# Two transformer layers on one core: the same instructions, put in order by the scheduler with its timeline simulation

## The chip, the core and the metric

The kernel runs on one core of a Trainium2 chip. The metric is the device time of one execution in microseconds (us), taken outside the profiler; less is better. A core has five engines that matter here: PE (matrix products; PEld is its loading of weights, which overlaps the products), DVE (vector work), ACT (activations and copies), POOL (general vector work) and SP, which here only issues DMAs. Each engine works through its own list of instructions strictly in order; an instruction that needs another engine's result waits for a semaphore, and everything behind it on its engine waits too.

## The reference

The input x holds 4 sequences (b) of 256 tokens with 256 features, in float32. Two layers follow, each an attention block and a feed-forward block with a residual:

```
x = x + attention0(layernorm(x))   # 16 query heads, 8 key/value heads of 128, RMS norm and rotary
                                   # embedding of q and k, causal with a window of 128
x = x + ffn0(layernorm(x))         # (silu(x Wg) * x Wu), the two largest of every four kept, then W_down; 1024 wide
x = x + attention1(layernorm(x))   # 16 heads of 128, causal
x = x + ffn1(layernorm(x))         # fwht(silu(x W1^T) * x W3^T) W2^T; fwht is a Walsh-Hadamard transform over 1024
```

All matrix products are in float32.

## The kernel before

The kernel is written in a framework of tiles: the program names buffers and emits instructions in the order in which its Python code runs; the framework finds out which instruction needs which, gives buffers of a pool out in turn, adds the waits, and **a scheduler orders the instructions of each engine** from an estimate of how long each takes. So the order on an engine is not the order of the code. Two things bind it besides the data: a buffer can only be written again when its readers are done, and `tc.issue_after(instruction)` keeps the instructions of a block behind one that the code names. Tiles carry the number of their buffer (sc_5554), which is the same in both programs. 

**Attention, both layers.** The work is cut into 16 units: in layer 0 unit n is sequence b = n // 4 and head group g = n % 4 (four query heads, two key/value heads); in layer 1 it is group n // 4 and sequence n % 4. `pipelined` (line 300 on) emits the stages of different units side by side: in layer 0 the seven stages project, rotate, turn, score, split, join, attend run 0, 0, 1, 2, 3, 4, 4 steps behind; in layer 1 project, score, attend run 0, 1, 2 behind. Each unit has two halves (kk), and each half goes through one chain:

- `sc`, the scores of two heads, on PE (L213, L214): a 128x128 and a 128x256 product for each head
- `p` and its row maxima `mx`, mask added, on DVE (L216); `nb`, the negative maxima scaled, on DVE (L221, L223)
- the exponential in place on ACT, four instructions (L226); `rs`, one over the row sums, on DVE (L231)
- four scalings of `p` by `rs` on POOL (L234), then `pl` on POOL (L240): the float32 words taken apart into planes of 16 bits, 128x1536
- `plT`, the planes transposed by a DMA that SP issues (L249); `pT`, the halves put together again on ACT and DVE (L260)
- `av` (line 268 and 271 in layer 1, 394 and 398 in layer 0) on PE; `zT`, its copy, on ACT (L731, L402)
- `po` on PE (L280 in layer 1, as `po1`; L292 in layer 0) and `x += po` on DVE (L286, L297)

In layer 0 the queries and keys come from `pj` on PE (L446); DVE multiplies by the rotary tables (`qs`, `qc`, L451) and adds (L469); ACT squares (L456), DVE sums (`ss`, L470); POOL makes `r`, the factor of the norm, with a power (L483 to L489), and scales k (`qc`, L492); PE turns k (`tr_k`, L518). The queries go to the scores turned by PE (`tr_q`, copied by DVE at L508) or, for later units, by DMA (`qpl` L240, `qplT` L480, put together by DVE into `qT` at L512). The layer norms are `bn_stats`, `bn_aggr` on DVE (L151, L152), a power on POOL (L157), `xn` on DVE (L171), and `tr_n` on PE (L182) or planes and a DMA transpose.

In layer 1 q, k and v come from `seven_products`: products of sums of 128-wide blocks, seven where plain blocks need eight. Each product (`qk_x`, `qk_y`, `qk_z`, L783; `v_x`, L789) is copied by ACT or summed by DVE (L654, L660, L663) before the same bank takes the next one.

**Feed-forward, both layers.** ffn0 makes gate and up (`pgu`, L550), keeps two of four on DVE (L569 to L583) and multiplies by W_down (`po_f`, L595). ffn1 makes both factors in the seven products (`gu_x`, `gu_y`, `gu_z`, L858), SiLU on ACT (L873), the product `h1` on DVE (L874), `po_f` (L595), then `x += po_f` (L604) and the output DMA.

The late part of layer 1's attention matters for the change. The output projections of units 9, 10, 11 and 13 (`po1` of the tiles 5577, 5588, 5650 and 5661) are not emitted at their turn but in the `attend` of units 14 and 15, behind the last projection:

```
        zTs, kept = {}, {14: (9, 10), 15: (11, 13)}

        def attend(n, held):
            ps, v = held
            for m in kept.get(n, ()):
                out(m, True)(zTs)
...
                    with tc.issue_after(last_of[1].ins):
                        project_out1(st([P, NT, D], "po1"), done[n], gw[g][2], b)
```

So PE has products at hand that need nothing more, which the scheduler may put where it likes behind the last projection. Unit 15's scores are sc_5524 and sc_5529 (p_5519) and sc_5549 and sc_5554 (p_5544); its two `av` are av1_5676 and av1_5685.

The change touches one line of `kernel`, where the framework's context is opened.

## Time and profile before

| | before |
|---|---|
| device time, 3 runs | 738.79, 738.90, 739.01 us; median 738.9 |
| span of the profiled execution, first to last instruction | 737.2 us |
| what lies around the span (median less span) | 1.7 us |
| granted PE clock, mean | 1.000 |
| PE, PEld busy | 725.0, 594.6 us |
| DVE, ACT, POOL busy | 469.2, 406.9, 345.0 us |

The profiled execution has no device time of its own beside its span; the runs' median less the span, 1.7 us, is taken as what lies around it. A PE that is busy is not a PE without loss: its matmuls are pipelined and a record's duration overlaps the next one, so the prediction goes by the distance from one start to the next. Two records stand in the trace for each float32 product, one for each transpose.

The stages of the kernel by time, from the trace: layer 0's attention to about 260 us, its feed-forward to about 360, layer 1's attention to about 655, its feed-forward to the end.

### The profile page before, as it was taken

Reading aid. Unit: us, or ns where it says so; the run is one execution under the profiler, and the core shown is the slowest. Engines: PE = TensorE matmul, PEld = TensorE weight load, DVE = VectorE, ACT = ScalarE, POOL = GpSimd, SP = SyncE. Lnnn points to the kernel's source line nnn. Section 1 sums busy time; section 2 is a strip of 40 time slices with the busy share of each in tenths; the row PEclk is TensorE's granted clock in tenths of the full one; section 3 lists DMA queues with packets and bytes.
Section 4 is the critical chain, followed back from the end, with each engine's and each line's share of the span. In section 5 each row is a group of like instructions: output and inputs, shape, how many; then the busy total and the mean of one; then the engine's idle time right before and its main releaser. Section 6 shows DMA issues by size and latency. Waiting matters only on the chain.

```text
span 737.2 us, 11593 instructions
## 1 busy us (share of the span) xinstructions
PE 725.0 (98%) x3912; PEld 594.6 (81%) x3912; DVE 469.2 (64%) x1402; ACT 406.9 (55%) x983; POOL 345.0 (47%) x489
## 2 busy tenths in 40 slices
PE   9999999999999999999999999999999999999998
PEld 5556576666666778888898999999998999899997
DVE  6999878888887537987655644464442655464443
ACT  2487887667767952222355555555556576434332
POOL 1588878897799631011116433343336575520000
PEclk9999999999999999999999999999999999999999
DMA  8732344425445545001324532342232223401100
GB/s 327 293 64 51 57 93 81 92 52 93 90 79 96 77 114 180 16 14 26 119 72 77 127 55 44 70 129 46 44 72 44 44 44 44 88 15 22 23 14 30
DMA packets 138348, 57.51 MB, mean 78 GB/s; under 512 B 131504, under 2 KB 133680, under 8 KB 137520
## 3 DMA queue, kind: packets, MB, share of 16 engines
q1 hardware_dynamic: 138288, 56.77, 33.9%
q8 instruction: 31, 0.51, 0.3%
q14 instruction: 29, 0.24, 0.1%
HBM read 22.94 MB, written 1.05 MB: 33 GB/s over the span
## 4 chain that ended last, share of the span: by engine, by line
PE 75%; DVE 9%; POOL 7%; issue 4%; ACT 3%; DMA 2%; SPq 0%; POOLq 0%; DVEq 0%; ACTq 0%
PE pj L446 10%; PE pgu L550 7%; PE po L292 7%; PE po_f L595 7%; PE qk_x L783 5%; PE po L280 5%; PE sc L214 5%; PE gu_x L858 4%; PE av L394 3%; PE qk_y L783 3%; PE v_x L789 3%; PE sc L213 3%; PE av L268 2%; POOL p L234 2%; PE gu_y L858 2%
## 5 line engine op out<-in xcount | busy, mean ns | idle before, releaser
L234 POOL TENSOR_SCALAR p<-p,rs 128x128 f32<-128x128 f32 (+1 forms) x256 | 115.4, 470 | 153.2 <-DVE rs L231 147.9
L240 POOL TENSOR_SCALAR pl<-p 128x1536 uint16<-128x1536 uint16 x64 | 94.3, 1474 | 4.8 <-POOL p L234 0.5
L260 ACT COPY pT<-plT 128x1536 uint16<-128x1536 uint16 (+1 forms) x60 | 86.2, 1494 | 11.5 <-DMA plT<-pl 11.5
L216 DVE CUSTOM_DVE_ANT_0 p<-sc,cst 128x128 f32<-128x128 f32 (+1 forms) x256 | 79.7, 351 | 10.5 <-PE sc L214 8.1
L226 ACT ACTIVATE p<-p,nb,r 128x128 f32<-128x128 f32 (+1 forms) x128 | 68.2, 535 | 20.2 <-DVE nb L223 20.2
L446 PE MATMUL pj<-wq,xnT 128*128 128x512 f32 x128 | 61.1, 595 | 1.1 <-DVE qT L508 1.1
L446 PE MATMUL pj<-wkv,xnT 128*128 128x512 f32 x128 | 60.1, 592 | 0.0
L226 ACT ACTIVATE p<-p,nb 128x128 f32<-128x128 f32 (+1 forms) x128 | 56.3, 447 | 4.0 <-DVE nb L221 4.0
L292 PE MATMUL po<-wo,zT 128*128 128x256 f32 x256 | 57.9, 379 | 0.0
L280 PE MATMUL po<-w_o,zT 128*128 128x256 f32 x256 | 57.6, 379 | 0.0
L456 ACT ACTIVATE sq<-pj 128x512 f32<-128x512 f32 (+1 forms) x64 | 30.9, 489 | 42.7 <-DVE qc L451 42.4
L292 PEld LDWEIGHTS po<-wo,zT 128*128 128x128 f32 x256 | 48.3, 190 | 7.0 <-ACT kT L519 0.6
L280 PEld LDWEIGHTS po<-w_o,zT 128*128 128x128 f32 x256 | 47.7, 190 | 6.0
L156 POOL TENSOR_SCALAR ve<-mv 128x2 f32<-128x2 f32 (+1 forms) x17 | 4.3, 253 | 97.5 <-DVE mv L152 97.0
L446 PEld LDWEIGHTS pj<-wkv,xnT 128*128 128x128 f32 x128 | 24.3, 190 | 30.2 <-issue 28.0
L451 DVE TENSOR_TENSOR qs<-pj,sin_s 128x512 f32<-128x512 f32 (+1 forms) x64 | 35.3, 551 | 13.5 <-PE pj L446 12.9
L446 PEld LDWEIGHTS pj<-wq,xnT 128*128 128x128 f32 x128 | 23.5, 190 | 24.2 <-issue 19.9
L666 ACT COPY qk<-qk_x 128x512 f32<-128x512 f32 x16 | 9.4, 587 | 58.1 <-PE qk_x L783 58.1
L268 PE MATMUL av<-pT,v 128*128 128x256 f32 x128 | 38.4, 382 | 1.2 <-DVE nb L221 1.1
L214 PE MATMUL sc<-kT,qT 128*128 128x256 f32 x128 | 38.3, 381 | 0.0
L214 PE MATMUL sc<-qk 128*128 128x256 f32 x128 | 38.2, 380 | 0.0
L240 POOL TENSOR_SCALAR qpl<-qc 128x1024 uint16<-128x1024 uint16 x20 | 28.8, 1453 | 18.9 <-PE av L398 8.2
(151 smaller groups left out, 1748.8 us busy)
## 6 DMA issues: line engine op xcount, KB each, us to landing
w<-in_w_dram SPq DMA_DIRECT2D x3, 1024.0 KB, 4.7
wq<-in_wq_dram SPq DMA_DIRECT2D x4, 512.0 KB, 7.6
wkv<-in_wkv_dram SPq DMA_DIRECT2D x4, 512.0 KB, 8.4
wo<-in_wo_dram SPq DMA_DIRECT2D x4, 512.0 KB, 10.2
w_qk<-in_w_q_dram SPq DMA_DIRECT2D x4, 512.0 KB, 5.2
w_qk<-in_w_k_dram SPq DMA_DIRECT2D x4, 512.0 KB, 6.1
w_v<-in_w_v_dram SPq DMA_DIRECT2D x4, 512.0 KB, 7.3
w_o<-in_w_o_dram SPq DMA_DIRECT2D x4, 512.0 KB, 6.0
```

What stands on the lines that cost most here:

```text
L214: nc.tensor.matmul(sc[:, P : 3 * P], lhsT=q[:, P:T], rhs=k, start=True, stop=True)
L216: last_of["mx"] = nc.vector.tensor_tensor_reduce(out=p[:, j, cols], in0=sc[:, cols], in1=mask[:, cols], scale=1.0, scalar=-3.0e38, op0=ALU ...
L226: last_of["exp"] = nc.scalar.activation(p[:, j, cols], p[:, j, cols], AF.Exp, bias=nb[:, j, i : i + 1], scale=SCALE1 if rq is None else rq ...
L234: nc.gpsimd.tensor_scalar(p[:, j, cols], p[:, j, cols], rs[:, j, i : i + 1], 1.0, ALU.mult, ALU.mult)
L240: last_of["planes"] = nc.gpsimd.tensor_scalar(o, i, 1.0, 1.0, ALU.mult, ALU.mult)
L260: copy(words.rearrange("p (n w) -> p w n", w=2), halves[:, :, js].rearrange("p w j n -> p w (j n)"),)
L268: nc.tensor.matmul(av, lhsT=v0, rhs=pT[:, 0:T], start=True, stop=False, skip_group_check=True)
L280: nc.tensor.matmul(po[:, t, :], lhsT=zT[:, j, t * P : (t + 1) * P], rhs=w[:, j, :], start=(t == j == 0), stop=(j == 3), skip_group_check=True,
L292: nc.tensor.matmul(po, lhsT=zTs[hd // 4][:, hd % 4, t * P : (t + 1) * P], rhs=w[:, hd, :], start=(hd == 0), stop=(hd == n - 1),)
L446: last_of[0] = nc.tensor.matmul(pj, lhsT=xnT[:, c, t * P : (t + 1) * P], rhs=w[:, g, c, :], start=(c == 0), stop=(c == NC - 1),)
L550: nc.tensor.matmul(o[:, j, :], lhsT=w[:, c, f0 + j, :], rhs=xnT[:, c, :], start=(c == 0), stop=(c == NC - 1),)
L783: last_of[1] = nc.tensor.matmul(o[:, j, :], lhsT=wqk[i - 1][:, j // 2, j % 2, :], rhs=x[i - 1], start=(first and j == 0), stop=True, skip_ ...
```

## The change

The scheduler is told to order the instructions with its own timeline simulation instead of its default estimate of durations.

```diff
-    with tile.TileContext(nc) as tc:
+    with tile.TileContext(nc, schedule_with_timeline_sim=True) as tc:
         two_layers(tc, *args)
```

The compiled programs hold the same instructions with the same buffers: 2026 on PE, 1402 on DVE, 727 on ACT, 492 on POOL, 136 on SP. Their order differs on every engine, and with it the waits: side by side, the two lists of PE differ in 1481 lines, those of DVE in 2253, of ACT in 1128, of POOL in 477 and of SP in 41. The blocks under `issue_after` stay behind the instructions that they name.

## The prediction

> **What bounds the kernel now.** I read the page's head first, then PE alone: the change moves instructions and removes none, so it can only add or remove time in which PE stands still.
>
> ```profile
> span 737.2 us, 11593 instructions
> ...
> PE 725.0 (98%) x3912; PEld 594.6 (81%) x3912; DVE 469.2 (64%) x1402; ACT 406.9 (55%) x983; POOL 345.0 (47%) x489
> ...
> PE 75%; DVE 9%; POOL 7%; issue 4%; ACT 3%; DMA 2%; SPq 0%; POOLq 0%; DVEq 0%; ACTq 0%
> ```
>
> PE is busy for 98%. Since a matmul's record overlaps the next, I count PE's need by starts, in the timeline of PE:
>
> ```profile
> 628.48 0.38 PE L213 MATMUL sc<-qk 128*128 128x128 f32 x2
> 628.70 0.60 PE L214 MATMUL sc<-qk 128*128 128x256 f32 x2
> 629.13 6.64 PE L280 MATMUL po<-w_o,zT 128*128 128x256 f32 x30
> ...
> 646.22 0.38 PE L271 MATMUL av<-pT,v 128*128 128x128 f32 x2
> 646.73 0.70 PE L268 MATMUL av<-pT,v 128*128 128x256 f32 x2
> ```
>
> Two records 128 wide take 0.22 us to the next start, two 256 wide 0.43; 646.22 to 646.73 is 0.51, a stall of 0.29. Over the trace the medians of one record are 0.112 (128), 0.216 (256) and 0.430 us (512 wide), and 1888 x 0.112 + 1695 x 0.216 + 328 x 0.430 = 718.6 us. The first matmul starts at 1.2, the last ends at 734.2. So 18.5 of 737.2 us are not PE's own work; gaps over 0.12 us number 20 and sum to 11.3. **About 10 us is all that any order could win.** Who ends the waits:
>
> ```profile
> PE av L394 <- DVE mx L216: 2.1, 3, 0.8
> PE tr_k L518 <- POOL qc L492: 2.0, 2, 1.6
> PE idle L140 <- DVE zeroes L137: 1.2, 1, 1.2
> PE pj L446 <- DVE qT L508: 1.1, 2, 0.9
> PE av L268 <- DVE nb L221: 1.1, 1, 1.1
> PE qk_x L783 <- DVE qk L663: 0.4, 1, 0.4
> ```
>
> (us in total, times, longest.) By place: 1.76 at 20.5 us; 1.4 at 37-49; 1.0 at 71; 0.4 at 82-84; 1.2 at 147-150; 2.3 at 217-254, the end of layer 0's attention; 1.8 at 363-396, the start of layer 1's; 0.3 at 646.
>
> [...]
>
> **The change, part by part.** I set PE's instructions one behind the other at these step times, without gaps, in each program's compiled order, and call the position T. Its end, 718.7, is the same in both. A stall appears where the chain behind a PE result needs longer than the PE work that stands before its user (its cover). For DVE, ACT and POOL, too, one instruction costs its distance to the next start where the trace has them back to back: L216 0.20 (128 wide) and 0.34 (256), L451 0.60 (512) and 0.33 (256), L469 0.87, L512 0.75, L226 0.38 and 0.49, the four of L234 1.6, L240 1.45. Between such places nothing is lost: in most of layer 0 the cover from pj to tr_k to sc to av grows by some us, ffn0 keeps its order, and in the middle units of layer 1 pT comes about 0.1 us late at worst, where before's own order gives 0.1 to 0.3 late by the same count without a gap in its trace. These, and PE's moved projections in ffn0, I take at nothing, covered by PE's 40.00 of each 40 us; if that cover is too thin, see the rivals. SP's queue I take at nothing too: its transposes keep their order behind the planes.
>
> 1. Start (T 0-60). One pj block (1.7 us) now stands between tr_q and tr_k, against the gap of 1.76. But bn_stats and bn_aggr of x4 to x7 (4 x 0.34 + 4 x 0.08 = 1.7 us) stand earlier on DVE, and DVE is the tight one there:
>
> ```profile
> 20.00:60.00 40.00, 37.29 (x155) 22.81 (x155) 38.75 (x108) 25.75 (x73) 27.99 (x38) 1.00 0.46 149
> ```
>
> (PE 37.29, then PEld, DVE 38.75 of 40 us.) DVE's worst lag behind PE grows from 5.4 to 6.4 us. Bounds -1.8 and +1.5; taken **+0.5**, nearest to DVE's lag.
>
> 2. 147-150. POOL has r and qc ahead of the scalings of p, and xn 4 us more: **-1.2** (bounds -1.2, 0).
>
> 3. The next batch's first score (sc_1645, T 155.3). It waits for qT_1564, two copies on DVE. Before, they stood right behind the row maxima. Now DVE has ahead of them the rotation of unit 10 and x2 += po_1585, and that po is the block that ends on PE at T 155.3. So after it: 0.1, the addition 0.42, the first copy 0.75: 156.6, +1.3. The other way round, DVE's sum from the last maximum at T 149.9 (2 x 0.87, 3.7 for eight L451, 0.2, then 0.42 and 0.75) gives 156.7. Taken **+1.4** (bounds +1.0, +2.3).
>
> 4. End of layer 0's attention. From the last score to its av 12.1 us of cover stand where 17.3 stood; the chain would end about 1.1 late, while the four gaps of 2.3 lose their cause, their pT copies being ahead. **-1.2** (bounds -2.3, +1.1).
>
> 5. Start of layer 1's attention. The pT copies get 2 to 4.5 us of cover: -1.8; three new tight places (0.1, 0.3, 0.1): **-1.3** (bounds -1.8, +1.0).
>
> 6. **End of layer 1's attention**, the term that decides. Positions T:
>
> ```
>                               before           after
> sc_5529 ends                  613.5            620.4
> sc_5554 (last score) ends     614.8            624.8
> po1_5650, last 7 products     within 623.9-627.4   621.1-624.1
> av1_5676 starts               630.9            630.9
> av1_5685 starts               632.2            632.2
> ```
>
> The free projections, which before stood between the last scores and their av, now stand ahead of the last scores. Cover from the last score to av1_5685 falls from 17.4 to 7.4 us. What the chain needs is shown by before's chain of waits (start, us):
>
> ```profile
> 636.63 1.47 POOL pl L240
> 638.11 1.61 POOL p L234 x4
> ...
> 641.88 3.72 DMA plT<-pl
> 645.60 0.02 issue
> 645.62 1.06 ACT pT L260
> 646.68 0.04 issue
> 646.73 0.70 PE av L268 x2
> ```
>
> Maxima 0.7, nb 0.15, four exponentials 1.85, rs 0.2, scalings 1.6, planes 1.5, transpose 3.7, copy 1.1: 10.8 from score to av, 3.4 more than the cover. The queues make it a little worse: on DVE rs_5523 stands behind x6 and x7 += po1_5650, which ends at T 624.1. So rs 624.9-625.1, scalings to 626.7, planes 628.2, transpose 631.9, copy 633.0: av1_5676 is 2.1 late. The second half: POOL free at 628.2, scalings 629.8, planes 631.3, transpose 635.0, copy 636.1: av1_5685 3.9 late in all. Behind the waiting av stand two projections, then ffn1; none can pass. Less the 0.3 that goes at 646: **+3.5** (bounds +2.0, +5.0).
>
> 7. Tail (T 708-713). Blocks of po_f that separated the last products are moved ahead. gu_x_6190's last product must wait for L663's reading of its bank (0.1 + 0.69 + issue, about 0.9), and po_f_6216 for h1_6182, whose copy 0.59, SiLU 1.06, the L663 ahead and product 1.23 end at T 713.0 against 711.8. Together **+1.2** (bounds 0, +1.5); before shows no gap here.
>
> Sum: 0.5 - 1.2 + 1.4 - 1.2 - 1.3 + 3.5 + 1.2 = +2.9. Span 737.2 + 2.9 = 740.1; with the 1.7 between span and median, **741.8 us**.
>
> [...]
>
> **Rivals.**
> A, faster: the order mends the queues of DVE and POOL. Every gap but the first start is ended by DVE, POOL or a pT copy; if all 10 us go and terms 3, 6 and 7 cost their 6.4, the time is 738.9 - 10 + 6.4 = 735.3. For it: terms 2, 4, 5 are seen to lose their cause. Against: at 37-84 (2.8 us) DVE is full, and more DVE work stands early there. It decides once over 7.9 us of the gaps go (6.4 plus the 1.5 of 0.2%).
> B, nothing that a measurement can tell (0.2%, 1.5 us): PE has 718.6 of work in any order, terms 1 to 5 give -1.8, and 6 and 7 give 3 instead of 4.7: 737.2 - 1.8 + 3 + 1.7 = 740.1. For it: PE's 98%. Against: term 6's chain has 3.4 us more than its cover without any queue.
> C, slower still: the order leaves nothing spare. In layer 1's dozen middle units the margin is about -0.1 us; if each half unit is 0.1 to 0.3 late, 24 x 0.2 = 5 us come on top: 746.6. For it: po moved ahead of where it covered; against: PE 40.00 of 40 there before, at like margins.
>
> **How the numbers follow.** Forecast with its own range (740.4 to 744.5) 0.42; C (to 749) 0.18; B 0.20; A (to 735) 0.20. The range takes the cases to 736.0, where half of A is left out, and to 749. Chances: faster by over 0.2% 0.20, within 0.2% 0.20, slower 0.60.
>
> **What would show it.** Right: a PE wait of 1.5 to 4 us at the last two av of L268 with plT and pT on the chain before it; a wait of about 1.4 at sc <- DVE qT L512; none left at tr_k, av L394 at 147-254 or at 363-396. Wrong: PE without a gap at the end of layer 1's attention (then POOL or the transpose took less than before's rows), or many small gaps at L268 between 400 and 600 us (C).

## The result, and the profile after

| | before | after |
|---|---|---|
| device time, median of 4 runs on the same chip | 738.95 us (738.79 to 739.58) | 762.42 us (760.17 to 764.21) |
| ratio, with its 95% interval | | 1.0316 [1.0291, 1.0341] |
| span of the profiled execution | 737.2 us | 758.9 us (its own device time 760.65) |
| granted PE clock, mean | 1.000 | 0.993 |

The change costs 23.5 us, 3.2%. The prediction was 741.8 us with a range of 736.0 to 749.0: the sign was right, but the time is 13.4 us beyond the upper end. The head of the page after the change:

```profile
span 758.9 us, 11520 instructions
...
PE 731.6 (96%) x3912; PEld 597.9 (79%) x3912; DVE 481.0 (63%) x1402; ACT 407.4 (54%) x983; POOL 357.4 (47%) x489
...
PE 78%; DVE 8%; POOL 4%; issue 3%; DMA 3%; ACT 3%; SPq 0%; POOLq 0%; ACTq 0%; DVEq 0%
```

PE still is the chain, with the same 3912 records, but its share is 96% where it was 98%. Who ended its waits (us in total, times, longest):

```profile
PE av L268 <- ACT pT L260: 3.9, 2, 2.3
PE tr_q L507 <- ACT sq L456: 2.4, 2, 2.0
PE tr_k L518 <- DVE mx L216: 2.3, 1, 2.3
PE sc L213 <- DVE qT L512: 2.2, 1, 2.2
PE sc L213 <- ACT zT L402: 1.8, 2, 1.2
PE tr_k L518 <- POOL p L234: 1.8, 1, 1.8
...
PE tr_n L182 <- DVE xn L171: 1.5, 1, 1.5
```

The first and the fourth of these lines are the two waits that the prediction named. The others it did not name, and three of them (tr_q, tr_k and sc waiting for sq, mx and zT) are of a kind that it had counted in its term 7 alone: sq, mx and zT are not data that the waiting product needs, they are the last readers of the PSUM bank into which it writes (a bank here is one of the buffers that the kernel's products are written into, from its PSUM pools `ps1`, `ps2` and `st_pool`).

**By place.** With the prediction's step times (T is a matmul's position if PE ran its own list without a gap), the lag is a matmul's start less its T. PE's work is the same in both kernels, so the difference of the lags shows where the time was lost:

| T, us | 20 | 40 | 60 | 80 | 100 | 140 | 160 | 220 | 260 | 350 | 400 | 600 | 635 | 660 | 718 |
|---|---|---|---|---|---|---|---|---|---|---|---|---|---|---|---|
| lag before | 5.6 | 6.0 | 7.2 | 8.8 | 8.8 | 9.8 | 10.1 | 10.8 | 12.8 | 12.7 | 14.7 | 14.3 | 14.7 | 15.2 | 15.3 |
| lag after | 4.5 | 9.5 | 14.5 | 20.9 | 22.4 | 22.4 | 25.4 | 25.3 | 29.8 | 29.7 | 31.2 | 31.1 | 35.7 | 35.9 | 37.0 |

At T 100 the changed kernel is already 13.6 us behind: the greater part of the loss is made in the first 100 us. The rest comes in four steps, at T 140 to 160, before 260, at 635 and in the tail. From 400 to 600, in layer 1's middle units, nothing is lost.

**What happens in the first 100 us.** PE's timeline after the change (start, duration, operation; the bracket at the end is the idle time before it and who ended it):

```profile
34.91 0.60 PE L214 MATMUL sc<-kT,qT 128*128 128x256 f32 x2
...
35.57 1.88 PE L446 MATMUL pj<-wkv,xnT 128*128 128x512 f32 x4
37.29 1.88 PE L446 MATMUL pj<-wq,xnT 128*128 128x512 f32 x4
39.00 1.88 PE L446 MATMUL pj<-wkv,xnT 128*128 128x512 f32 x4
40.72 0.39 PE L213 MATMUL sc<-kT,qT 128*128 128x128 f32 x2
...
47.37 0.41 PE L518 MATMUL tr_k<-cst,qc 128*128 128x128 f32 x2 [2.27 <-DVE mx L216]
```

Three scores of unit 0 end with the one at 34.91; the fourth (sc_376) comes at 40.72, behind three projections of unit 3. Before, the four scores stood together at 32 to 35 us. PE itself loses nothing here. But DVE, whose list is as strict, now stands still twice:

```profile
36.66 0.16 DVE L223 SCALAR_TENSOR_TENSOR nb<-mx,r 128x4 f32<-128x4 f32 x1
39.18 0.18 DVE L231 RECIPROCAL rs<-sm 128x4 f32<-128x4 f32 x1 [2.36 <-ACT p L226]
41.58 0.29 DVE L216 CUSTOM_DVE_ANT_0 p<-sc,cst 128x128 f32<-128x128 f32 x1 [2.22 <-PE sc L214]
```

First it waits 2.36 us with `rs` at its head, for exponentials that ACT has only begun; then 2.22 us with the row maximum of the fourth score at its head. Up to three finished projections, which want to be rotated (L451), stand behind both. Before, the row maxima of the fourth score and two additions (L469) stood between `nb` and `rs`, and DVE had no gap there. DVE is the tight engine of this stretch, so it does not make the 4.6 us good. PE pays later: at 47.37, where tr_k waits 2.27 us for a PSUM bank that a row maximum still has to read, then at 59 and at 87 to 92. The same pattern returns with units 4 and 8: sc_928 stands behind pj_1008 and pj_1014, with 2.36 us of idle DVE at `rs` and 1.34 at the row maximum, and sc_1532 behind pj_1621, with 1.65 us at the row maximum. Unit 4's place, at 98 to 102 us, comes after most of the loss: at T 80, before its score starts at 101.3, the kernel is already 12.1 us behind.

**The clock joins in.** The windows of the same trace (window, length, then busy time of PE, PEld, DVE, ACT and POOL, the granted clock, DMA share, GB/s):

```profile
20.00:60.00 40.00, 35.14 (x138) 20.25 (x136) 35.42 (x94) 17.18 (x55) 22.35 (x31) 1.00 0.41 142
60.00:70.00 10.00, 8.19 (x26) 4.74 (x27) 8.74 (x28) 10.00 (x25) 9.74 (x15) 0.83 0.20 38
...
90.00:100.00 10.00, 8.23 (x30) 6.04 (x31) 6.33 (x17) 4.44 (x15) 4.90 (x5) 0.66 0.42 79
```

In the stretch where before had PE busy for 37.29 of 40 us and DVE for 38.75, PE now has 35.14 and DVE 35.42. And the clock falls to 0.50, from 63.5 to 66.9 and from 90.8 to 97.6 us by the trace's clock record. Before the first stretch PE has gaps of 1.92, 0.30 and 0.55 us, around the start of the second 2.15 and 1.70. In the second stretch a pair 256 wide has 0.85 us to the next start (at 93.34), where 0.43 is usual, and a pair 128 wide 0.43 (at 92.91), where 0.22 is; the two stretches cost 1.7 and 2.6 us on top of the gaps (the distances between starts there, less the step times). The four runs of this kernel (760.65, 764.19, 760.17, 764.21 us) differ in the same way: their mean clocks are 0.993, 0.986, 0.995 and 0.986, which is some 470 us for one unit of clock. By that slope, an estimate from four runs, about 4.7 of the 23.5 us are half clock and 18.8 are waits.

**At the end of layer 1's attention**, which the prediction made its deciding place:

```profile
664.51 0.70 PE L268 MATMUL av<-pT,v 128*128 128x256 f32 x2 [2.27 <-ACT pT L260]
...
667.76 0.70 PE L268 MATMUL av<-pT,v 128*128 128x256 f32 x2 [1.68 <-ACT pT L260]
```

From start to start the two gaps are 2.44 and 1.84 us, at the two av that were named. The chain before the first of them (start, duration, what):

```profile
656.49 1.64 POOL p L234 x4
658.13 0.08 issue
658.20 1.37 POOL pl L240
...
659.70 3.67 DMA plT<-pl
663.38 0.02 issue
663.40 1.07 ACT pT L260
664.47 0.04 issue
664.51 0.70 PE av L268 x2
```

Scalings, planes, transpose and copy stand on it as foretold. The maxima and `nb` end at 653.8; between them and the scalings the profile's chain runs over a power on POOL, but POOL's scalings waited for `rs`, which came at 656.22, behind the exponentials (653.93 to 655.80) and the additions to x (L286) on DVE, as the prediction had it.

### The profile page after: what moved, and what is told of

Its sections match the earlier page's. It is cut to its first block, busy times and chain, and to the rows that moved or that the text cites. A ratio compares the mean times of both kernels' runs of the same rounds, so it can differ in the third digit from the quotient of the medians.

```text
span 758.9 us, 11520 instructions
## 1 busy us (share of the span) xinstructions
PE 731.6 (96%) x3912; PEld 597.9 (79%) x3912; DVE 481.0 (63%) x1402; ACT 407.4 (54%) x983; POOL 357.4 (47%) x489
## 4 chain that ended last, share of the span: by engine, by line
PE 78%; DVE 8%; POOL 4%; issue 3%; DMA 3%; ACT 3%; SPq 0%; POOLq 0%; ACTq 0%; DVEq 0%
PE pj L446 11%; PE po_f L595 7%; PE pgu L550 7%; PE qk_x L783 7%; PE po L280 6%; PE sc L214 6%; PE gu_x L858 4%; PE po L292 4%; PE av L268 3%; PE qk_y L783 3%; PE v_x L789 3%; PE sc L213 3%; PE v_zy L789 2%; PE av L394 2%; DMA plT<-pl 2%
## 5 line engine op out<-in xcount | busy, mean ns | idle before, releaser
L234 POOL TENSOR_SCALAR p<-p,rs 128x128 f32<-128x128 f32 (+1 forms) x256 | 126.3, 510 | 145.2 <-DVE rs L231 89.6
L240 POOL TENSOR_SCALAR pl<-p 128x1536 uint16<-128x1536 uint16 x64 | 96.7, 1515 | 6.4 <-DMA plT<-pl 2.3
L260 ACT COPY pT<-plT 128x1536 uint16<-128x1536 uint16 (+1 forms) x60 | 86.2, 1491 | 12.7 <-DMA plT<-pl 12.7
L286 DVE TENSOR_TENSOR x<-po,x 128x256 f32<-128x256 f32 x32 | 12.1, 418 | 57.1 <-PE po L280 57.1
L446 PEld LDWEIGHTS pj<-wq,xnT 128*128 128x128 f32 x128 | 23.3, 190 | 25.4 <-issue 19.4
L456 ACT ACTIVATE sq<-pj 128x512 f32<-128x512 f32 (+1 forms) x64 | 29.8, 487 | 23.4 <-DVE qc L451 21.8
L451 DVE TENSOR_TENSOR qs<-pj,sin_s 128x512 f32<-128x512 f32 (+1 forms) x64 | 34.7, 543 | 6.5 <-PE pj L446 6.4
L260 DVE COPY pT<-plT 128x768 uint16<-128x768 uint16 (+1 forms) x36 | 25.7, 718 | 18.7 <-DMA plT<-pl 18.7
```

Source lines behind the costliest of these rows:

```text
L234: nc.gpsimd.tensor_scalar(p[:, j, cols], p[:, j, cols], rs[:, j, i : i + 1], 1.0, ALU.mult, ALU.mult)
L240: last_of["planes"] = nc.gpsimd.tensor_scalar(o, i, 1.0, 1.0, ALU.mult, ALU.mult)
L260: copy(words.rearrange("p (n w) -> p w n", w=2), halves[:, :, js].rearrange("p w j n -> p w (j n)"),)
L446: last_of[0] = nc.tensor.matmul(pj, lhsT=xnT[:, c, t * P : (t + 1) * P], rhs=w[:, g, c, :], start=(c == 0), stop=(c == NC - 1),)
```

## The experiments

Two explanations of the first 100 us were set against each other: that the one score parted from its sisters, and what the scheduler set around it, holds up DVE, and that the new order is too tight as a whole in layer 0 (more DVE work early, less slack everywhere), so that no single place matters. For the end of layer 1's attention the prediction's account (too little cover behind the last score) stood against the same general tightness. The comparisons are with the kernel before on the same chip.

### The new order in layer 0's attention alone (blk_plain, blk_l0sim)

```diff
-    attention0()
+    with tc.block(schedule_with_timeline_sim=False):   # blk_plain; blk_l0sim: True
+        attention0()
```

Both start from the kernel before; a block makes the scheduler order its instructions by themselves.

> Control: layer 0's attention stands in a block of its own, ordered by the default estimate like the rest. PE's order is that of before but for 16 matmuls at the start of the feed-forward. Both theories: 738.9 us within 1.5 (a block costs each engine one jump); were it more than 2 us over, the next run would have to be read against this one and not against before.

Measured: 763.24 us against 737.67, 1.0350 [1.0335, 1.0365].

> The timeline order for layer 0's attention alone; the rest has the default order. Theory 1 (the loss is local: PE stands still where the new order makes it): the lag of PE behind its own work was 17.0 us larger in the changed kernel than before at the end of layer 0's attention, so 739 + 17 = 756, and the two late stalls (2.4 and 1.8 us at the last av) are gone. Rival (the stalls of the start are caused by what the scheduler moves in from later stages, or by the clock alone): under 748.

Measured: 784.48 us, 1.0631 [1.0615, 1.0647].

The control failed as a control. PE's order in blk_plain is that of before but for 16 matmuls, yet the block brought another order to DVE's list. DVE's waits in the first 32 us of blk_plain:

```profile
DVE st L151 <- DMA x<-in_x_dram: 18.5, 3, 11.0
```

The bn_stats of x4 to x7 stand at DVE's head before their loads have come, 18.5 us in all; PE is 15 us later than before at T 20 already, and about 7 more are lost where the block ends. Within layer 0's attention (T 20 to 260) the lag grows by 10.1 us in blk_plain and by 21.1 in blk_l0sim (7.2 before, 25.3 after), and the two late av at the end of layer 1 are gone in the latter. So the new order of layer 0's attention costs time by itself, but the 11 us are a difference of two disturbed kernels: the size stays inconclusive, and the block is no clean way to test a part.

### The parted scores put back (pin_start)

From the kernel after; the projections of units 3 and 7 (three of each unit's four blocks) are kept behind the last score emitted so far, that of units 0 and 4.

```diff
-            nc.tensor.matmul(sc[:, P : 3 * P], ...)
+            last_of["sc"] = nc.tensor.matmul(sc[:, P : 3 * P], ...)
...
-                last_of[0] = nc.tensor.matmul(pj, ...)
+                with tc.issue_after(last_of["sc"].ins) if late_pj and (t or n == 2) else nullcontext():
+                    last_of[0] = nc.tensor.matmul(pj, ...)      # late_pj = n in (3, 7)
```

> The changed kernel with one order undone: the projections of units 3 and 7 stay behind the last score of units 0 and 4, as before the change. Theory 1: DVE, the tight engine, stood idle 4.6 us at 36.8 to 41.6 us and 3.7 us at 98 to 102 us, each time with a row maximum at its head whose score PE had put behind three projections; PE paid for it at 44.7, 59 and 87 to 97 us, and the clock's loss came with these gaps. Then most of the 13.6 us that T 0 to 100 lost come back: 762 to 750, with the clock near 1.00. Rival (ACT's and POOL's queues make the loss: the squares behind two pT copies, the power behind late sums): only the gap at 44.7 goes, 762 to 759.

Measured: 751.87 us (750.11 to 754.68), 1.0196 [1.0167, 1.0224]. The lag at T 100 is 10.7 us, where after has 22.4 and before 8.8: **11.7 of the 13.6 us come back from two units' projections**, the two long waits of tr_k vanish, and tr_q's shrink from 2.4 to 0.8. An order that is too tight as a whole would not mend at two places. Of the 11.7 us, 10.2 are back by T 80, ahead of unit 4's parted score, so that unit 7's projections can have brought no more than about 1.5. The scheduler ordered the other engines anew as well: in DVE's list `rs` of unit 0 now stands behind two rotations, and DVE's longest wait there is 0.71 us. So the run shows that these projections' place, with what the scheduler set around it, made the loss; how much was the score's wait and how much that of `rs` it does not show. What is left stands at the head of this kernel's list of PE waits:

```profile
PE av L268 <- ACT pT L260: 3.9, 2, 2.3
PE av L394 <- DVE pT L260: 2.3, 1, 2.3
PE sc L213 <- DVE qT L512: 2.3, 1, 2.3
```

The second line, at the end of layer 0's attention, was 1.4 us in the profile after the change. The pin is not shown to have lengthened it: it is 2.3 us in the profile of pin_end below too, which has the order of after in layer 0.

### The last scores of layer 1 kept ahead of the free projections (pin_end)

From the kernel after; `last_of["sc"]` as above.

```diff
-                    with tc.issue_after(last_of[1].ins):
+                    with tc.issue_after(last_of["sc"].ins):
                         project_out1(st([P, NT, D], "po1"), done[n], gw[g][2], b)
```

> The changed kernel with the four kept output projections of layer 1 held behind the last score of unit 15. Theory 1 (their place alone made the two waits at the last av, 2.4 and 1.8 us): both go, 762.4 to 758.3. Rival (POOL, the transposes and DVE's queue make them, wherever the projections stand): they stay above 2 us together, and the time within 2 us of the changed kernel.

Measured: 761.43 us, 1.0317 [1.0296, 1.0337]: nothing won. Both late av are in time now, as the account by cover has it. But an earlier one, of unit 13 (av1_5493, which the expectation of pin_four calls unit 14's), is late instead, on PE:

```profile
640.99 0.70 PE L268 MATMUL av<-pT,v 128*128 128x256 f32 x2 [3.20 <-ACT pT L260]
...
643.88 1.06 PE L268 MATMUL av<-pT,v 128*128 128x256 f32 x2
```

and on ACT before it:

```profile
639.40 0.50 ACT L226 ACTIVATE p<-p,nb 128x256 f32<-128x256 f32 x1
639.89 1.95 ACT L260 COPY pT<-plT 128x768 uint16<-128x768 uint16 x2
```

The free projections had also covered unit 13's av. Without them it is PE's turn before its pT copy is made, which stands in ACT's list behind the exponentials of unit 14 that end at 639.9. The gap of 3.4 us was also followed by half clock (the 1.06 us of the second PE line, where 0.60 is usual; the mean clock from 640 to 650 us is 0.83), 1.7 us more. Cover is a stock: the same projections can stand ahead of one av or of the other. The account by cover was right on where the stall comes from; that moving them would win its 4 us was wrong.

### The pins added one by one (pin_three, pin_four, pin_five)

pin_three starts from pin_start, and each of the others holds what the one before it holds. pin_three: also unit 11's projections behind unit 8's last score, and `x2 += po` behind the copies of qT. pin_four: also three kept units of layer 1 (10, 11 and 13) behind the last score, while that of unit 9 stays free to cover unit 13's av. pin_five: also layer 0's kept output projections of sequence 2, second half, and of sequence 3 behind unit 15's last score.

```diff
+    late_pj = n in (3, 7, 11)                                              # pin_three
+    with tc.issue_after(last_of["qT"].ins) if (b, t) == (1, 0) else nullcontext():
+        nc.vector.tensor_tensor(xs[b * NT + t], po, xs[b * NT + t], ALU.add)
...
-                    with tc.issue_after(last_of[1].ins):                    # pin_four
+                    with tc.issue_after(last_of["sc" if n > 9 else 1].ins):
...
-                        with tc.issue_after(last_of[0].ins):                # pin_five
+                        with tc.issue_after(last_of[0 if b == 2 and t == 0 else "sc"].ins):
```

> As the run with the projections of units 3 and 7 behind the last scores of units 0 and 4, and two more orders undone: unit 11's projections behind unit 8's last score, and x2 += po behind the qT copies that unit 9's first score waits for. Theory 1 (a score kept from its sisters by projections, and an addition at DVE's head that waits for the block PE works on): the wait at sc <- DVE qT L512 (2.4 us, with the half clock behind it 2.5 more in that run) goes to under 0.7, and the time falls from 751.9 by 2.4 to 4.5, to 747.4 to 749.5. Rival (the eight rotations of unit 11 ahead of the copies on DVE are enough): 1.5 us or more of the wait stays, 750.5 or more.

Measured: 747.42 us against 738.75, 1.0125 [1.0104, 1.0146]. The wait at sc <- qT is gone: from T 140 to 160 the lag does not grow (10.81 to 10.78).

> As the run before this one, and at the end of layer 1's attention the kept projections of units 10, 11 and 13 behind the last score, unit 9's left where the timeline order put it. Holding all four had moved the wait to unit 14's av1_5493, whose pT copy stood on ACT behind the next exponentials, and made it 3.4 us. Theory 1 (it is a matter of cover: unit 9's block of 3.45 us in front of that av, and 14.4 us between the last score and the last av where the chain needs 10.8): the two waits of 2.4 and 1.9 us fall to under 1 us together, 4 us less than the run before this one. Rival (ACT's queue is late whatever stands on PE): over 2.5 us of waits at L268 between T 605 and 633.

Measured: 746.28 us, 1.0106 [1.0090, 1.0121]. The two late av shrink from 4.3 us to one of 1.2, but a new wait comes at the place where the scores now stand close together:

```profile
636.36 0.49 PE L213 MATMUL sc<-qk 128*128 128x128 f32 x2 [1.49 <-DVE x L286]
```

`x += po` (L286) does not make anything that a score reads; it is the last reader of the PSUM bank. The medians of pin_three and pin_four, on one chip, differ by 1.1 us where 4 were expected. That wait itself was not taken away in a run.

> As the run with unit 9's block left in place, and at the end of layer 0's attention the kept projections po_2508, po_2518 and po_2541 behind unit 15's last score. Theory 1 (the same shape as at the end of layer 1: the free products stand ahead of the last scores, so the last chain has too little cover): the wait of 2.4 us at the last av of L394 goes to under 0.5, and the time from 746.3 to 743.9. Rival (DVE's copy pT_2539 or the banks that zT frees set it): over 1.5 us stay, at that av or moved to another.

Measured: 743.49 us (742.74 to 743.66) against 738.72, 1.0062 [1.0047, 1.0077]; its clock is 1.000 in all runs, and the wait of 2.3 us at av L394 is gone. So the pins together bring the 23.5 us down to 4.8. What remains is small and spread: about 2.0 us in the first 100 (tr_n waits 1.3 for xn, tr_q 0.8 for sq's bank), 2.9 at the end of layer 1 and 1.0 in the tail, less the gains at T 100 to 160.

### What a stall costs (stall_one, stall_two)

From the kernel before; unused work is added in ffn0, and nothing is left out: POOL raises a small tile to a power once or twice (2.3 us each), a small product reads it, and the next gate products are kept behind that product.

```diff
+            if n == 3:
+                z = small.tile([P, 12], F32, tag="z", name="z")
+                nc.gpsimd.tensor_scalar(z, h[:, 0, 0:12], 0.0, 1.0, ALU.mult, ALU.add)
+                for _ in range(1):                         # stall_two: 2
+                    nc.gpsimd.tensor_tensor(z, z, mhalf, ALU.pow)
+                last_of["stall"] = nc.tensor.matmul(bank([12], "stall"), lhsT=zeroes[:, 0:P], rhs=z, ...)
...
+                    with tc.issue_after(last_of["stall"].ins) if wait else nullcontext():
                         nc.tensor.matmul(o[:, j, :], ...)
```

> The kernel before in its default order, with a chain added that the computation does not use: POOL makes 128x12 ones from h of ffn0's fourth half and takes one power (2.3 us), a small product on PE reads the result, and the fifth half's pgu products stand behind it. PE, else busy without a gap there, stands still once for some 2.5 us. Theory (a gap costs its own length, and above some 2 us sometimes the half clock behind it): 738.8 + 2.5 = 741.3, up to 743 in runs whose clock is under 1.00. Rival (a gap costs only its length): 741.3 in every run.

Measured: 743.50 us against 738.72, 1.0064 [1.0049, 1.0079]. PE's timeline:

```profile
308.78 3.62 PE L604 MATMUL po_f<-w_down,h 128*128 128x256 f32 x16
314.71 0.39 PE L534 MATMUL stall<-z,zeroes 128*128 128x12 f32 x2 [2.31 <-POOL z L533]
314.95 5.39 PE L559 MATMUL pgu<-xnT,w_gate 128*128 128x256 f32 x16
320.18 3.62 PE L559 MATMUL pgu<-xnT,w_up 128*128 128x256 f32 x16
```

Sixteen records 256 wide take 3.62 us before the gap and after it, but 5.39 right behind it: a gap of 2.47 us cost 2.47 + 1.77 of half clock. The mean clock was 0.998 in each of the four runs, so this is no accident of one execution.

> The same with two powers: one gap of some 4.8 us. Theory: its length and always a stretch at half clock, 1.5 to 2.5 us more: 738.8 + 4.8 + 2 = 745.6. Rival (length alone): 743.6 with the clock at 1.00. In both runs the default order of what comes behind may differ a little from before's; the lag of PE is read at the gap.

Measured: 747.35 us, 1.0112 [1.0095, 1.0129].

```profile
318.48 0.60 PE L534 MATMUL stall<-z,zeroes 128*128 128x12 f32 x2 [4.86 <-POOL z L533]
318.93 6.23 PE L559 MATMUL pgu<-xnT,w_gate 128*128 128x256 f32 x16
```

From start to start the gap is 5.02 us, and the sixteen records behind it take 6.23 us where 3.62 are usual: 2.6 us of half clock (the mean clock is 0.86 from 310 to 320 us and 0.80 from 320 to 330). Twice the gap did not cost twice the half clock, 2.6 us against 1.77.

### The other way: a wait of the kernel before taken away (act_half, act_all)

The prediction gave the waits at the start of layer 1's attention as winnable. From the kernel before, the second half of unit 0's pT copies goes to ACT in place of DVE (act_half), or both halves (act_all).

```diff
-                        (nc.vector.tensor_copy, slice(0, 1), None) if n < 1 else
+                        (nc.scalar.copy, slice(0, 1), None) if n < 1 else                # act_all only
...
-                    (nc.vector.tensor_copy, slice(1, 2), last_of["sum"]),
+                    (nc.scalar.copy if n < 1 else nc.vector.tensor_copy, slice(1, 2), last_of["sum"]),
```

> The kernel before, in its default order, with one copy moved: the second half of unit 0's pT in layer 1 goes to ACT, which is idle from 392.3 to 397.8 us, and not to DVE, where it stood behind the sums of the next block and a row maximum until 397.2 us. Expected: the gap of 1.23 us at 396.5 goes, 738.9 to 737.7; if ACT's copy delays the exponentials behind it, nothing is won.

Measured: 738.80 us in 11 runs against 738.75, 0.9998 [0.9990, 1.0007]: nothing. The gap of 1.0 us stayed, since the copy of the second av's first half was still on DVE, behind the sums of L631.

> The kernel before in its default order, with all four copies of unit 0's pT in layer 1 on ACT. With one half moved, the gap at 396.5 us stayed (1.0 of 1.2 us), since the av that waited, the second one, still had its first half on DVE behind the sums, done at 397.7. Expected: the copies run on ACT one after the other from 392.7 to 396.7, so the gap falls to 0.3 us or less: 738.8 to 738.0. If the second av, which now stands earlier on PE, waits for ACT instead, nothing is won.

Measured: 736.98 us in 11 runs against 737.74 in 15, 0.9989 [0.9980, 0.9998]. The gap is gone (the lag from T 380 to 400 grows by 0.5 us and not 1.3), and 0.8 us is won (the interval reaches from 0.02% to 0.20%). It is the fastest kernel here; of the 10 us in which the prediction saw PE stand still, this is the only piece that a run here won, by taking away one wait of a microsecond by hand.

## Why the prediction was wrong, step by step

| step | predicted | measured (by lag) |
|---|---|---|
| 1, start (to T 100) | +0.5 (-1.8 to +1.5) | **+13.6** |
| 2, 147 to 150 us | -1.2 | -1.2 |
| 3, sc_1645 | +1.4 (+1.0 to +2.3) | +2.9 |
| 4, end of layer 0's attention (T 160 to 350) | -1.2 (-2.3 to +1.1) | +1.7 |
| 5, start of layer 1's attention (T 350 to 400) | -1.3 | -0.4 |
| 6, end of layer 1's attention (T 400 to 660) | +3.5 (+2.0 to +5.0) | +4.1 |
| 7, tail (to the end) | +1.2 (0 to +1.5) | +1.0 |
| sum | +2.9 | +21.7 |

The measured column is the profiled execution, whose span grew by 21.7 us; the medians differ by 23.5.

**Step 1 failed**, together with the sentence that between the named places nothing is lost. Of the 18.8 us that the sum is short, 13.1 are here: 7.3 by T 60, the stretch that the step was worked out for, less its 0.5, and 6.3 more by T 100, which it did not look at. The step compared sums: DVE's work against PE's, and the chains of data. It saw rightly that DVE is the tight engine there. But a tight engine that works in order is not only late by its work: it can wait at its head. Where one score was set behind three ready projections, PE lost nothing at once and DVE 4.6 us, 2.2 at that score's row maximum and 2.4 at `rs` just ahead of it; and pin_start shows that this pattern in two units was 11.7 of the 13.6 us, the half clock that followed included. The prediction took a longer cover ("the cover from pj to tr_k to sc to av grows") as a sign that nothing is lost; it looked at what PE has to wait for and not at what DVE has to.

**Steps 3 and 4** had places and mechanisms but missed a kind of wait. Step 3's gap is 2.4 + 0.5 us; DVE had been idle for 1.65 us some 8 us before it, waiting for the parted score of unit 8 (sc_1532). pin_three took the gap away with two edits together, the score's and the addition's, so the share of each is not known. In step 4 the wait at pT is 1.5 us, near the 1.1 foretold; another 2.1 come from scores that wait for zT (L402), which frees their bank. A wait for a bank stands in no chain of data, and in layer 0 the prediction counted only such chains; the one bank that it did count, in step 7, came as foretold.

**Step 5** lost its gap at the first pT copies, as foretold, but its three new tight places cost 0.3, 0.7 and 0.4 us where 0.5 in all was counted.

**Step 6** was right in mechanism and size, 2.1 and 1.8 against the measured 2.4 and 1.8 us in two pieces, and so was step 7 by its size. So the sign of the forecast was right for a small part of the loss: 4.1 of 21.7 us stand where the prediction saw the deciding term, and 13.6 where it saw 0.5. What pin_end adds is that this was not a loss that one edit can take back.

The clock was the other thing that the sum left out: no term of it has half clock, and before shows none, with a clock of 1.00 and no PE gap over 1.76 us behind its first projections. After the change two clusters of gaps (1.92 + 0.30 + 0.55, and 2.15 + 1.70 us) were followed by half clock; the single gaps of 2.4 us at 45 and 178 us and the two of step 6 (2.44 and 1.84) were not: the clock is 1.00 from 40 to 50, 170 to 190 and 650 to 700 us. It followed the single gaps of 2.47 us in stall_one, 5.02 in stall_two and 3.4 in pin_end. Behind step 3's gap of 2.4 us, where after kept its clock, pin_start lost 2.5 us to half clock, as the expectation of pin_three has it. So in these runs the length of a gap alone did not settle it; what does was not shown.

The rivals: A and B needed layer 0 to win or to stay even. C, slower by some 5 us more, had the direction, but put it into layer 1's middle units, where the lags from T 400 to 600 change by -0.4 us before and -0.1 after.

**What stays open.** Why the timeline simulation sets the fourth score behind projections cannot be read from a trace. The reverse test, parting one score in the kernel before, was not tried. The 2 us that pin_five still loses in the first 100 were not taken apart. Nor was it measured what the longer instructions cost: the same 1402 instructions on DVE were busy for 481.0 us after the change where they took 469.2 before, those on POOL for 357.4 and 345.0, so prices read from the rows of before do not all hold in another order. pin_start has DVE at 477.1 and POOL at 358.7 with most of the first loss gone, so this was not the main part of it.

## What to carry to other kernels

The runs are of one kernel; what they suggest is this. When a scheduler or an edit reorders a kernel whose bound engine is full, first look for members of a group (here one of four scores) that now stand behind ready work, and ask which engine has the group's consumer at the head of its list: that engine's idle time, not its summed work, is the price, if it is tight there. Count the release of a buffer as a wait like any other. Take a stall away only after asking what the covering work covers besides, since it can come back at the next list, and price a PE gap at its length and, where half clock follows, at more: 1.77 us behind the 2.47 of stall_one, 1.7 behind the 3.4 of pin_end, 2.6 behind the 5.02 of stall_two, 1.7 and 2.6 behind the two clusters after the change.

## What the runs showed of the hardware that was not expected

- Half clock followed a PE gap of 2.47 us in stall_one, whose mean clock is 0.998 in all four runs, and cost 1.77 us beyond it. None followed the 2.4 us at 178 us after the change (clock 1.00 from 170 to 190 us).
- After the change the clock was 0.50 for 3.41 us from 63.49 and for 6.83 us from 90.80. In stall_one it was 0.50 for 3.41 us, from 315.12 to 318.53 (stall_one's windows: busy time of PE, PEld, DVE, ACT and POOL, then the clock):

```profile
311.71:315.12 3.41, 1.10 (x7) 0.67 (x6) 3.31 (x8) 1.06 (x1) 2.48 (x2) 1.00 0.00 0
315.12:318.53 3.41, 3.41 (x9) 2.66 (x9) 3.38 (x15) 0.00 (x0) 0.00 (x0) 0.50 0.00 0
318.53:321.94 3.41, 3.41 (x18) 3.00 (x17) 0.85 (x3) 1.02 (x1) 2.12 (x4) 1.00 0.00 0
```

- The time of one kernel then varied with its mean clock: 760.2 us at 0.995 to 764.2 at 0.986 after the change, where before has 738.8 to 739.6 (1.000 in its profiled execution), and pin_five 742.7 to 743.7 at 1.000 in all four runs.
- The order of work that needs a load mattered as much as that of products: bn_stats at the head of DVE's list waited 18.5 us in all for their loads in blk_plain, and PE, with almost the list of before, was 15 us later by T 20; that is the greater part of the 3.5% that this kernel is slower.
